# A third kind of first quartic, and one round more between a moved tile's way back and its product

## The chip, the cores and the metric

The kernel runs on one core of one Trainium2 chip. The metric is the device time of one execution in microseconds (us). A core has five engines that each run their own list of instructions in order: the matrix engine (PE; its weight loads are shown apart as PEld), the vector engine (DVE), the scalar engine (ACT), GpSimd (POOL) and SyncE (SP). They wait for each other on semaphores. DMA transfers are issued here from SP and from ACT; the profile shows these issuers as SPq and ACTq.

## The reference, cut to what matters

The input x is 32 images of 32 channels of 128 x 128 numbers in f32. The first layer adds to x the square root, by five Newton steps, of every normalised channel matrix; the second adds a spectral convolution that keeps 32 x 32 modes at two corners.

```python
def _L0_conv_ref(A):
    A2 = A.reshape(b_s * c, n_c, n_c)
    normA = jnp.sqrt(jnp.sum(A2 * A2, axis=(1, 2)))
    Y = A2 / normA[:, None, None]
    Z = jnp.broadcast_to(I, A2.shape)
    for _ in range(5):
        T = 0.5 * (3.0 * I - jnp.matmul(Z, Y))
        Y = jnp.matmul(Y, T)
        Z = jnp.matmul(T, Z)
    return (Y * jnp.sqrt(normA)[:, None, None]).reshape(b_s, c, n_c, n_c)
...
x = x + _L0_conv_ref(_gn(x))
x = x + _L1_conv_ref(_gn(x), L1_conv_weights1, L1_conv_weights2)
```

`_gn` normalises each pair of channels of an image. `_L1_conv_ref` takes the real part of a 2D Fourier transform, mixes 32 input into 32 output channels with a weight for each mode, and transforms back. Most of the matrix work is the first layer: 1024 channel matrices.

## The kernel before, in words

**Sets.** Four channels of an image are a set, so there are 32 x 8 = 256 sets, worked off in order. A set's tile is 128 x 512 (four matrices side by side) and fills one PSUM bank. The kernel holds each matrix and its transpose (`m` and `mb`, loaded as tiles x and b by `fetch`, scaled by `staged`), because PE multiplies the transpose of its first operand.

**Quartics.** Two Newton steps together are a polynomial of degree four, a quartic, in the matrix. `newton` runs, for a set: a first quartic q, y = q times the matrix, the new matrix m = y times q, a second quartic of it, two products with that, a last step t, and a last product that DVE adds to the tile xt. A quartic needs a product, some combination with multiples of the identity, and a second product, whose operands need one more transposition.

There are two ways to get it. `near_quartic` transposes on PE (a matmul with the identity, `transposed`) and uses POOL's sum r = mb + eye; DVE combines PSUM and SBUF into v and w. `far_quartic` has *moved tiles*: DVE transposes 32 x 32 blocks on the way out of PSUM (`turned`, tile turn), and DMAs then put the blocks into their places: `across` with four DMAs of 64 KB inside SBUF, into w; or `away` to DRAM and `back`, one DMA of 256 KB each way. The product reads the result through `by_rows`, in rearranged rows. POOL makes the differences `eye - matrix`. A far set does 10 products of four channels and no PE transposition; a near set does 8 of these, 4 double-width matmuls (`both`) and 3 transpositions of four channels (v twice, m once). Images 1 to 18 are far, image 0 and images 19 (`FIRST`) to 31 are near.

**The order.** The main loop goes in rounds. There are 9 lanes; a lane holds a set's `newton`, a generator, and is advanced by one section, up to its next `yield`, in each round. So a `yield` in a set is one round of the other sets' work between two of its steps. `rest` is two rounds. A new set starts in a free lane when `due` allows, every `FAR` or `NEAR` rounds; near sets also need `room`, under `LESS` = 5 in flight. Once a round the loop also advances the other queues: `preps` (statistics for the normalisation, from xs_in), `posts` (store the finished set to `mid`, the folded sums, the second normalisation), `specs` and `prods` (forward transform and mode products, by groups of 20, 7, 3 and 2 images) and `backs` (the inverse: load `mid` as yt, add, store to out). The order written this way is kept on every engine.

**Buffers.** `rooms` gives for each tag the number of buffers for the whole kernel and of additional ones that exist until `change()`, after `MORE` = 158 sets, gives their memory to the mode products and the inverse. In the late part only the first number is left. When a buffer is used again, its new writer waits for the last reader.

**DMA queues.** `fetch` issues the two loads of a set on SP for far images and on ACT for near ones. Statistics loads are on ACT. Stores to mid and out, loads of yt, spectra and weights, and all moved tiles are on SP. `store` issues out stores whenever it is called and something lies in `stores`, put there by `unfold`, which issues POOL's additions to yt.

All instructions go through one wrapper, so the profile gives line 88 for each: they are told apart by tile names (ps is PSUM).

Of the kernel before, what the change touches and what calls it, by code (L numbers as in the profile page):

```python
# [38 lines left out]
C = 32  # L39
G = 16  # L40
LANES, LESS = 9, 5
FAR, NEAR = 26 / 9, 25 / 5
GROUPS = (20, 7, 3, 2)


# [3 lines left out]
MS = 1 / QR  # L49
# [44 lines left out]
def conv_preact_kernel(  # L94
# [49 lines left out]
        od.append(dram.tile(shape, F32, name=f"od{i}", tag=f"od{i}"))  # L144
    where = [(i, b) for i, n in enumerate(GROUPS) for b in range(n)]

    stp = ctx.enter_context(tc.tile_pool(name="stp", bufs=4))
    up = ctx.enter_context(tc.tile_pool(name="up", bufs=1))
    sp = ctx.enter_context(tc.tile_pool(name="sp", bufs=1))
    small = ctx.enter_context(tc.tile_pool(name="small", bufs=1))  # L150
# [28 lines left out]
    def bank():  # L179
        return ps8.tile([P, 4, P], F32, tag="ps", name="ps")  # L180
# [41 lines left out]
    def prep(bs, made):  # L222
# [5 lines left out]
        tiles = []  # L228
        parts = [(b, i) for b in bs for i in range(C // 4)]

        ahead = 3 if first_b else 8

        def load(k):
            b, i = parts[k]
# [70 lines left out]
        yield  # L305


    rooms = dict(b=(4, 6), xt=(10, 5), x=(3, 2), r=(4, 0), v=(3, 2), w=(3, 2), q=(4, 2))
    rooms.update(my=(4, 3), mb=(2, 4), t=(3, 2), y4=(2, 2), turn=(0, 4))
    turns = dict.fromkeys(rooms, 0)  # L310

    def four(tag, more):
# [44 lines left out]
    def is_far(b):  # L357
        return 0 < b < FIRST
# [16 lines left out]
    def staged(b, g, nm, sc, off, sn):  # L375

        m = four("x", has_more(b, g))
        xt, mb = raw.pop((b, g))

        def on_scalar(t, x, offset, scale, c):  # L380
            c = slice(c, c + 1)
            kept(
                nc.scalar.activation(t, x, AF.Identity, bias=offset[:, c], scale=scale[:, c])
            )

        for j in range(4):
# [20 lines left out]
    def near_quartic(m, mb, more):  # L407


        v = plus(m, -QA * MS, products(mb, m), "v", more)  # L410
        yield
        r = four("r", more)
        nc.gpsimd.tensor_tensor(r, mb, eye, ALU.add)
# [22 lines left out]
        kept(nc.sync.dma_start(out=into, in_=src))  # L436
        return t

    def by_rows(t):
        return blocks(t).rearrange("p a c j -> p c a j")  # L440

    def across(t, more):

        w = four("w", more)
# [7 lines left out]
            )  # L452
        return w

    def far_quartic(m, mb, v, f, later, more):
# [6 lines left out]
        if later:  # L462
# [12 lines left out]
        return q  # L475

    rest = (None, None)

    def newton(g, sn, xt, m, mb, v, far, more):


        qf, et, eye_t = (QS, EYE_Q, eye_q) if far else (QF, EYE, eye)
        if far:
            q = yield from far_quartic(m, mb, v, 1.0, False, more)
        else:
            q = yield from near_quartic(m, mb, more)
        my = four("my", more)
# [23 lines left out]
        else:  # L511
# [2 lines left out]
            mb = taken(transposed(m), "mb", more)  # L514
            yield from rest
            q = yield from near_quartic(m, mb, more)
            both = [bank().rearrange("p (j k) x -> p j k x", k=2) for _ in range(2)]
            for j in range(4):
                nc.tensor.matmul(both[j // 2][:, j % 2], q[:, j], my[:, j], start=True, stop=True)
# [223 lines left out]
    def small_products(i):  # L743
# [121 lines left out]
    def weights():  # L865


        kinds = [("b", 2)] * 3 + [("x", 2), ("b", 4), ("x", 4), ("x", 10)]
        kinds += [("my", 11)] * 2 + [("r", 12)] * 3 + [("mb", 15)] * 2 + [("v", 15)] * 2
        kinds += [("w", 16)] * 2 + [("my", 16), ("r", 17), ("v", 18)] + [("q", 19)] * 3  # L870
# [69 lines left out]
    def unfold():  # L940

        while sums:
            b, o, y, d = sums.pop(0)
            engine = nc.vector if tail and o % 16 else nc.gpsimd
            for half, op in enumerate((ALU.subtract, ALU.add)):
                yh = y[:, :, 64 * half : 64 * half + 64]
                engine.tensor_tensor(yh, yh, d, op)
            stores.append((b, o, y))

    placed = {}  # L950

# [180 lines left out]
    while todo or any(lanes) or posts or specs or prods or backs:  # L1132
# [3 lines left out]
        for i in range(LANES):  # L1136
# [1 line left out]
            step(loads)  # L1138
            far = todo and is_far(todo[0][0])
            under_way = [is_far(lane[0]) for lane in lanes if lane]  # L1140
            room = far or under_way.count(False) + 0.6 * under_way.count(True) < LESS
            if lanes[i] is None and todo and room and rounds >= due:
                due = max(due, rounds - 1) + (FAR if far else NEAR)
                while norms:
                    step(norms)
                b, g = todo.pop(0)
                xt = ready[0][0]
                lanes[i] = (b, g, xt, newton(g, made[b][3], *ready.pop(0), far, has_more(b, g)))
                if stages:
                    stage()  # L1150
                if not todo:
# [89 lines left out]
```

## Time and profile before

| | |
|---|---|
| median of 3 runs | 2969.88 us (2962.28 to 2977.81) |
| the profiled execution, its own time | 2972.83 us |
| its span, first to last instruction | 2971.0 us |
| instructions | 74,313 |
| granted PE clock, mean | 0.987 |
| HBM traffic | 402.42 MB read, 229.11 MB written |
| DMA issues on SP for moved tiles | 288 away, 144 + 144 back, 576 across |

Read along the time axis, the page has four parts. The first 100 us start up with image 0. To about 1500 us the far sets run with almost nothing beside them but statistics and forward transforms. From 1500 us the near sets of images 19 to 31 share the engines with mode products and with the inverse of the first images. After 2850 us the last mode products and inverses run out. Busy shares of each engine by slice stand in the page's second part:

```profile
PE   7999999999999999999999999999999999999995
...
DVE  7779788888788888888886645886787766777565
ACT  3555555555555555555544445555555544655552
POOL 4677777776767777777665534877778764678453
DMA  5687878787787878787843566767767747766577
```

### The profile page before, as it was taken

What the parts mean: (1) busy time and instruction counts of PE and PEld (TensorE: products, weight loads), DVE (VectorE), ACT (ScalarE), POOL (GpSimd) and SP (SyncE); (2) the same over time, 40 slices, a digit from 0 to 9 for tenths busy, and PEclk for the clock granted to TensorE, in tenths of its full rate; (3) what the DMA queues carried; (4) which work ended last, traced back from release to release, by engine and by line L of the source; (5) the groups of instructions that cost most, each with busy time, mean ns of one, the idle gap of its engine ahead of it and who ended that gap; (6) DMA issues with size and microseconds to landing.
All of it is one profiled execution on the core that took longest, in us unless ns stands there. A gap on an engine that the chain in (4) does not pass through costs nothing.

```text
span 2971.0 us, 74313 instructions
## 1 busy us (share of the span) xinstructions
PE 2847.8 (96%) x27688; PEld 2666.9 (90%) x27688; DVE 2270.9 (76%) x4407; ACT 1544.7 (52%) x3899; POOL 1986.9 (67%) x2308
## 2 busy tenths in 40 slices
PE   7999999999999999999999999999999999999995
PEld 7899999998999999999999889888888999888983
DVE  7779788888788888888886645886787766777565
ACT  3555555555555555555544445555555544655552
POOL 4677777776767777777665534877778764678453
PEclk9999999999999999999999999999999999999997
DMA  5687878787787878787843566767767747766577
GB/s 174 185 250 244 242 242 251 240 257 231 233 252 217 275 228 263 236 253 239 270 145 98 164 209 210 269 217 271 269 228 268 273 127 222 218 223 225 180 221 260
DMA packets 553078, 674.22 MB, mean 227 GB/s; under 512 B 99344, under 2 KB 333840, under 8 KB 552720
## 3 DMA queue, kind: packets, MB, share of 16 engines
q1 hardware_dynamic: 480576, 536.53, 56.9%
q10 hardware_dynamic: 72144, 132.94, 14.3%
q8 instruction: 222, 3.64, 0.5%
q14 instruction: 136, 1.11, 0.1%
HBM read 402.42 MB, written 229.11 MB: 213 GB/s over the span
## 4 chain that ended last, share of the span: by engine, by line
PE 66%; POOL 11%; DMA 9%; issue 7%; DVE 5%; ACT 1%; SPq 1%; ACTq 0%; DVEq 0%; POOLq 0%
PE ps L88 66%; POOL yt L88 3%; POOL r L88 3%; POOL x L88 2%; DMA w<-turn 2%; POOL fold L88 2%; DMA yt<-mid 1%; DMA b<-in_x 1%; DMA xt<-in_xt 1%; SPq L88 1%; DVE turn L88 1%; DMA xs<-in_xs 1%; DVE yt L88 1%; DMA mid<-xt 1%; DMA out<-yt 1%
## 5 line engine op out<-in xcount | busy, mean ns | idle before, releaser
L88 ACT ACTIVATE my<-ps 128x512 f32<-128x512 f32 x512 | 305.3, 600 | 563.6 <-PE ps L88 443.7
L88 POOL TENSOR_TENSOR fold<-xt 128x256 f32<-128x256 f32 x512 | 363.5, 732 | 285.9 <-DVE xt L88 257.2
L88 ACT ACTIVATE b<-b,a_off,a_sc 128x128 f32<-128x128 f32 x1024 | 469.8, 493 | 97.1 <-issue 15.9
L88 PE MATMUL ps<-my,q 128*128 128x128 f32 (+1 forms) x2944 | 474.4, 309 | 5.7 <-ACT my L88 3.8
L88 PEld LDWEIGHTS ps<-my,q 128*128 128x128 f32 x2944 | 412.9, 192 | 33.0 <-ACT my L88 4.6
L88 POOL TENSOR_TENSOR v<-eye_v,b 128x512 f32<-128x512 f32 x144 | 183.6, 1275 | 382.9 <-ACT b L88 344.6
L88 POOL TENSOR_TENSOR yt<-yt,d 128x512 f32<-128x512 f32 x244 | 306.8, 1281 | 187.4 <-ACT d L88 155.3
L88 PE MATMUL ps<-w,v 128*128 128x128 f32 x2944 | 399.9, 279 | 13.0 <-DVE w L88 10.6
L88 PEld LDWEIGHTS ps<-w,v 128*128 128x128 f32 x2944 | 363.5, 194 | 22.3 <-issue 7.6
L88 DVE STREAM_TRANSPOSE turn<-ps 128x512 f32<-128x512 f32 x432 | 299.7, 702 | 62.2 <-PE ps L88 57.1
L88 ACT ACTIVATE t<-ps 128x256 f32<-128x256 f32 (+1 forms) x368 | 171.0, 467 | 333.3 <-PE ps L88 316.7
L88 POOL TENSOR_SCALAR x<-xt,a_nm,a_sc 128x128 f32<-128x128 f32 x736 | 321.2, 450 | 15.8 <-DVE a_sc L88 15.5
L88 ACT ACTIVATE y<-ps,a_t_s 128x128 f32<-128x128 f32 x1024 | 291.4, 371 | 45.2 <-PE ps L88 45.1
L88 PE MATMUL ps<-q,t 128*128 128x128 f32 x2048 | 273.8, 277 | 0.8 <-DVE v L88 0.8
L88 DVE SCALAR_TENSOR_TENSOR w<-ps,r 128x512 f32<-128x512 f32 x224 | 153.1, 684 | 139.3 <-POOL r L88 71.2
L88 PEld LDWEIGHTS ps<-q,t 128*128 128x128 f32 x2048 | 249.6, 192 | 3.3 <-issue 1.2
L88 DVE BATCH_NORM_STATS2 a_st<-xs 128x6 f32<-128x256 f32 x504 | 185.9, 410 | 64.9 <-DMA xs<-in_xs 64.6
L88 DVE SCALAR_TENSOR_TENSOR q<-ps,eye 128x512 f32<-128x512 f32 x224 | 153.3, 684 | 97.6 <-PE ps L88 94.8
L88 DVE TENSOR_TENSOR xt<-ps,xt 128x512 f32<-128x512 f32 x256 | 174.7, 683 | 40.7 <-PE ps L88 35.2
L88 POOL TENSOR_TENSOR r<-mb,eye 128x512 f32<-128x512 f32 x112 | 142.9, 1276 | 91.8 <-ACT mb L88 91.8
L88 DVE TENSOR_TENSOR yt<-ps,yt 128x512 f32<-128x512 f32 x256 | 163.3, 681 | 39.9 <-PE ps L88 34.4
L88 POOL TENSOR_TENSOR my<-eye_q,my 128x512 f32<-128x512 f32 x144 | 183.8, 1277 | 7.5 <-PE ps L88 7.5
(147 smaller groups left out, 6284.9 us busy)
## 6 DMA issues: line engine op xcount, KB each, us to landing
turn<-turn SPq DMA_DIRECT2D x288, 256.0 KB
mid<-xt SPq DMA_DIRECT2D x256, 256.0 KB
yt<-mid SPq DMA_DIRECT2D x128, 512.0 KB
xs<-in_xs ACTq DMA_DIRECT2D x252, 256.0 KB
out<-yt SPq DMA_DIRECT2D x115, 512.0 KB
b<-in_x SPq DMA_DIRECT2D x144, 256.0 KB
xt<-in_xt SPq DMA_DIRECT2D x144, 256.0 KB
w<-turn SPq DMA_DIRECT2D x576, 64.0 KB
```

The costliest lines, as they stand in the source:

```text
L88: return self.tc.keep_in_program_order(issue(*args, **kw))
```

## The change

In words: images 19 to 31 get `late_quartic` as their first quartic, with a moved tile instead of the PE transposition (`across`, read five rounds later); their second quartic stays near. The way back in a far set's second quartic is issued four rounds instead of three ahead of its product, and `FAR` goes from 26/9 to 27/9. POOL's sum in `near_quartic` is issued in the section before. Late sets are fetched on SP, half of their m is scaled on ACT instead of POOL, six may be in flight, and out stores are issued two rounds or more after their additions. The buffers are shared out anew; statistics are loaded five tiles ahead instead of three.

```diff
-FAR, NEAR = 26 / 9, 25 / 5
+FAR, NEAR = 27 / 9, 25 / 5
...
-    stp = ctx.enter_context(tc.tile_pool(name="stp", bufs=4))
+    stp = ctx.enter_context(tc.tile_pool(name="stp", bufs=6))
...
-        ahead = 3 if first_b else 8
+        ahead = 5 if first_b else 8
...
-    rooms = dict(b=(4, 6), xt=(10, 5), x=(3, 2), r=(4, 0), v=(3, 2), w=(3, 2), q=(4, 2))
-    rooms.update(my=(4, 3), mb=(2, 4), t=(3, 2), y4=(2, 2), turn=(0, 4))
+    rooms = dict(b=(5, 5), xt=(10, 4), x=(3, 2), r=(3, 0), v=(3, 2), w=(3, 2), q=(3, 3))
+    rooms.update(my=(3, 4), mb=(2, 4), t=(2, 3), y4=(2, 2), turn=(2, 2))
...
     def fetch(b, g):
-        queue = nc.sync if is_far(b) else nc.scalar
+        queue = nc.sync if b else nc.scalar
...
-            if j < 2 or not is_far(b):
+            if j < 2 or not b:
...
     def near_quartic(m, mb, more):
-        v = plus(m, -QA * MS, products(mb, m), "v", more)
-        yield
         r = four("r", more)
         nc.gpsimd.tensor_tensor(r, mb, eye, ALU.add)
+        v = plus(m, -QA * MS, products(mb, m), "v", more)
+        yield
         yield
         w = plus(transposed(v), 1.0, r, "w", more)
...
+    def late_quartic(m, mb, more):
+        v = minus(eye_v, m, four("v", more))
+        ps = products(mb, m)
+        t = turned(ps, more)
+        yield
+        nc.vector.scalar_tensor_tensor(v, ps, 1 / (9 * MS), v, ALU.mult, ALU.add)
+        w = across(t, more)
+        yield
+        minus(eye_q, mb, mb)
+        yield from rest
+        yield from rest
+        q = plus(products(v, by_rows(w)), 9 / (39 * MS**2), mb, "q", more)
+        yield from rest
+        return q
...
     def far_quartic(m, mb, v, f, later, more):
...
         if later:
             w = back(held, "w", more)
-            yield
+            yield from rest
         yield from rest
...
         if far:
             q = yield from far_quartic(m, mb, v, 1.0, False, more)
+        elif late:
+            q = yield from late_quartic(m, mb, more)
         else:
             q = yield from near_quartic(m, mb, more)
...
         for k2 in range(len(xks)):
             load_spectra(k2)
+        yield from rest
...
     def store():
-        while stores:
-            b, o, y = stores.pop(0)
+        while stores and (tail or rounds - stores[0][3] >= 2):
+            b, o, y, _ = stores.pop(0)
...
-            room = far or under_way.count(False) + 0.6 * under_way.count(True) < LESS
+            less = LESS if any(under_way) else LESS + 1
+            room = far or under_way.count(False) + 0.6 * under_way.count(True) < less
...
             if i == 3 or tail:
                 step(posts)
+            if i == 0:
+                store()
```

Left out are the passing on of `late`, the constants that go with it (QS and EYE_Q for the first half of a late set, QF and EYE after), and a new list of slots into which `weights` loads the last weights as buffers come free.

More of the change, by code (lines that the diff above doesn't have):

```diff
@@ L407, in near_quartic @@
     def near_quartic(m, mb, more):
+        r = four("r", more)
+        nc.gpsimd.tensor_tensor(r, mb, eye, ALU.add)
         v = plus(m, -QA * MS, products(mb, m), "v", more)
         yield
-        r = four("r", more)
-        nc.gpsimd.tensor_tensor(r, mb, eye, ALU.add)
         yield
@@ L437, in back @@
         return t
-    def by_rows(t):
-        return blocks(t).rearrange("p a c j -> p c a j")
     def across(t, more):
@@ L453, in across, with by_rows @@
         return w
+    def by_rows(t):
+        return blocks(t).rearrange("p a c j -> p c a j")
+    def late_quartic(m, mb, more):
[12 more added lines that the diff above has]
+        return q
     def far_quartic(m, mb, v, f, later, more):
@@ L459, in far_quartic @@
             held = away(turned(ps, more))
+            yield
         else:
             w = across(turned(ps, more), more)
-        if later:
-            yield
         nc.vector.scalar_tensor_tensor(v, ps, 1 / (9 * MS), v, ALU.mult, ALU.add)
@@ L477, in conv_preact_kernel, with newton @@
     rest = (None, None)
-    def newton(g, sn, xt, m, mb, v, far, more):
-        qf, et, eye_t = (QS, EYE_Q, eye_q) if far else (QF, EYE, eye)
+    def newton(g, sn, xt, m, mb, v, far, late, more):
+        qf, et, eye_t = (QS, EYE_Q, eye_q) if far or late else (QF, EYE, eye)
         if far:
             q = yield from far_quartic(m, mb, v, 1.0, False, more)
+        elif late:
+            q = yield from late_quartic(m, mb, more)
         else:
@@ L516, in newton @@
             q = yield from near_quartic(m, mb, more)
+            qf, et, eye_t = QF, EYE, eye
             both = [bank().rearrange("p (j k) x -> p j k x", k=2) for _ in range(2)]
@@ L865, in weights @@
     def weights():
-        kinds = [("b", 2)] * 3 + [("x", 2), ("b", 4), ("x", 4), ("x", 10)]
-        kinds += [("my", 11)] * 2 + [("r", 12)] * 3 + [("mb", 15)] * 2 + [("v", 15)] * 2
-        kinds += [("w", 16)] * 2 + [("my", 16), ("r", 17), ("v", 18)] + [("q", 19)] * 3
+        kinds = [("b", 3)] * 3 + [("x", 3), ("b", 6), ("x", 6), ("b", 10), ("x", 12)]
+        kinds += [("my", 13)] + [("r", 14)] * 2 + [("mb", 17)] * 2 + [("v", 17)] * 2
+        kinds += [("w", 18)] * 2 + [("my", 18), ("r", 19), ("v", 20), ("y4", 21)] + [("q", 21)] * 2 + [("q", 23)]
         first = B * C // 4 - 10
@@ L947, in unfold @@
                 engine.tensor_tensor(yh, yh, d, op)
-            stores.append((b, o, y))
+            stores.append((b, o, y, rounds))
     placed = {}
@@ L1147, in conv_preact_kernel @@
                 xt = ready[0][0]
-                lanes[i] = (b, g, xt, newton(g, made[b][3], *ready.pop(0), far, has_more(b, g)))
+                lanes[i] = (b, g, xt, newton(g, made[b][3], *ready.pop(0), far, b >= FIRST, has_more(b, g)))
                 if stages:
```

## The prediction

> **What bounds the kernel now.** I read the page's busy times first, then stages of the span, then the timeline of the matrix engine alone, then the waits.
>
> ```profile
> PE 2847.8 (96%) x27688; PEld 2666.9 (90%) x27688; DVE 2270.9 (76%) x4407; ACT 1544.7 (52%) x3899; POOL 1986.9 (67%) x2308
> ...
> PE 66%; POOL 11%; DMA 9%; issue 7%; DVE 5%; ACT 1%; SPq 1%; ACTq 0%; DVEq 0%; POOLq 0%
> ```
>
> PE is busy nearly all the time, and the chain of waits that ended last lies on it for two thirds. Matmuls overlap, though, so 96% may hide slack. The stages (length; then busy PE, PEld, DVE, ACT, POOL; granted clock, DMA share, GB/s) and a stretch of PE alone:
>
> ```profile
> 100.00:1500.00 1400.00, 1362.79 (x12287) 1318.56 (x12286) 1173.71 (x2303) 756.90 (x1929) 1023.89 (x1138) 0.99 0.80 244
> 1500.00:1900.00 400.00, 391.66 (x4071) 361.66 (x4071) 257.87 (x511) 191.59 (x476) 204.97 (x274) 1.00 0.55 175
> 1900.00:2850.00 950.00, 924.53 (x9851) 842.89 (x9850) 695.51 (x1294) 505.36 (x1278) 663.24 (x784) 0.99 0.68 225
> ```
>
> ```profile
> 2254.83 1.16 PE L88 MATMUL ps<-y,t 128*128 128x128 f32 x8
> 2255.82 1.06 PE L88 MATMUL ps<-my,mb 128*128 128x128 f32 x8
> 2256.71 0.60 PE L88 MATMUL ps<-ident,v 128*128 128x128 f32 x4
> 2257.15 2.78 PE L88 MATMUL ps<-my,q 128*128 128x256 f32 x16
> ```
>
> Read the starts, not the lengths. A four-channel product is 8 records (two for each f32 matmul) and the next group starts 0.89 us later, 0.112 a record. A transposition of four channels is 4 records and takes 0.44 us. If each record is charged its usual start-to-start step, of the 2971 us some 166 are left that are not matrix work: 63 in 100 to 1500 us (images 1 to 18), 18 in 1500 to 1900, 47 in 1900 to 2850, the rest at start and end. PE works through its list with 4 to 5% of gaps in either main stage, so work taken from it should come off the end time.
>
> What the gaps are:
>
> ```profile
> DVE w L88 <- POOL r L88: 71.2, 35, 5.6
> ...
> PE ps L88 <- DMA w<-turn: 17.2, 11, 5.2
> ```
>
> (us in total, times, longest.) The first is DVE waiting for POOL's sum in the near quartics; the late products of w and v lose 13.1 us against their usual step. The second is PE itself, waiting for a moved tile. It falls on products that read w and r, the second quartic of the far sets; with the shorter gaps that go by other names, those products lose 26.5 us between 100 and 1500 us.
>
> **The change, part by part.**
>
> *First quartic of images 19 to 31.* It drops one transposition: 13 images x 8 sets x 4 = 416 transposing matmuls.
>
> ```profile
> L88 PE MATMUL ps<-ident,v 128*128 128x128 f32 x896 | 137.9, 277 | 4.5 <-DVE xt L88 2.3 <-DVE v L88 2.2
> L88 POOL TENSOR_SCALAR x<-xt,a_nm,a_sc 128x128 f32<-128x128 f32 x736 | 321.2, 450 | 15.8 <-DVE a_sc L88 15.5 <-DMA xt<-in_xt 0.3
> L88 ACT ACTIVATE x<-xt,a_off,a_sc 128x128 f32<-128x128 f32 x288 | 143.6, 499 | 9.5 <-DVE xt L88 2.5 <-DMA mb<-turn 2.4 <-DVE v L88 2.3
> L88 POOL TENSOR_TENSOR v<-eye_v,b 128x512 f32<-128x512 f32 x144 | 183.6, 1275 | 382.9 <-ACT b L88 344.6 <-PE ps L88 35.8 <-ACT b_r L88 2.5
> L88 DVE STREAM_TRANSPOSE turn<-ps 128x512 f32<-128x512 f32 x432 | 299.7, 702 | 62.2 <-PE ps L88 57.1 <-DMA w<-turn 1.1 <-DMA mb<-turn 0.2
> L88 DVE SCALAR_TENSOR_TENSOR w<-ps,r 128x512 f32<-128x512 f32 x224 | 153.1, 684 | 139.3 <-POOL r L88 71.2 <-PE ps L88 57.8 <-POOL x L88 8.5
> ```
>
> The 277 ns are the length of one, overlapping its neighbours; the starts give 0.109, so 416 x 0.109 = 45 us off PE. Bounds: 50 (the mean step with waits is 0.119), and 0 if PE were not the bound. I take -45. The product that stays reads its moving operand in rearranged rows; the far sets' products do so already at the same 0.112, so nothing is added.
>
> The Trainium skill (TensorE: Matmul & The Clock Gate, Part 4: PE-mode transpose) gives about 275 ns for a 128x128 transposition inside a kernel, the length that this row shows too. By it the part would bring 416 x 0.275 = 114 us; the starts, which decide, bring 45.
>
> Per late set the other engines get: POOL two differences of 1.275 for one sum of 1.276 and two scalings of 0.450 fewer, +0.375 us, 39 us over 104 sets; ACT two scalings, +1.0 us; DVE a transposition (0.702) and a combination (0.65) for two combinations (0.682 and 0.684), nothing. In 1900 to 2850 us POOL is busy for 0.70, ACT 0.53, DVE 0.73; idle time covers all three. If it did not, the POOL part would cost up to 39 us.
>
> SP gets four issues of 64 KB per late set (their issue lasts 0.594 us at the median in the far stage, 2.4 us a set of 13) and the two loads of a set that ACT's queue had (statistics loads stay on ACT's). What is queued behind on SP is the store of the finished set, the y loads and stores of the inverse, and late weights. The DMA engines get 512 pieces of 512 bytes. In the far stage such a piece takes 29 ns, so 512 x 29 / 16 = 0.93 us a set, 0.07 on a share of 0.68: 0.75, still under the 0.80 of the far stage.
>
> The Trainium skill (DMA: Bandwidth & Descriptors, Rules for kernel authors) speaks against this: many small transfers should be coalesced, and its bandwidth table (Measured) has 0.95 us for 64 KB. By that, four would fill the DMA engines for 3.8 us of a set's 13 and bring the share to 0.97, where every late load waits; the pieces in the trace are four times cheaper, and the page's own next section limits the penalty of small pieces to HBM.
>
> *Is the moved tile there in time?* The product stands five rounds behind its issue. Adding PE's records (at the steps above) in the built order between issue and product gives 8.9 us at least and 11.0 at the median. In the far stage of the trace before, pieces of w landed, counted from their place in the order, after 6.6 us (half), 9.9 (90%), 11.5 (98%), 13.5 (last); issue lag on SP is in it. A few late sets wait some 2 us: +4, from 0 to 45.
>
> *Way back of the far sets, 27 rounds.* The product goes from three rounds behind the issue to four. The same count: median from 9.8 to 11.6 us, the shortest 2% from 6.5 to 9.8. Against the landings above, the 10% that came too late become about 2%. Of 26.5 us I take 15 back; bounds 0 (the wait reappears elsewhere) and 26.5. A lane is held one round longer, 28 for 27, so nine lanes start a set every 3.1 rounds instead of 3.0; a round has no work of its own, so PE's list is as long as before. DVE-fed products come slightly closer (median of the nearest 4.9 for y and q in both).
>
> *Second quartic's sum on POOL one section earlier; shorter late rounds.* The sum is now two rounds ahead of its reader: up to 13 us back. But a late round holds less PE work: late products with a DVE or ACT producer 1.5 to 3 us ahead rise from 73 to 266. In the trace before, products at 2 to 3 us lost 0.02 us each, those at 3 to 4 us 0.08: 193 x 0.08 = 15 us at most. In the first quartic DVE's combination now waits for POOL's difference, one round behind it, as it waited for the sum; queued behind it on DVE are the other sets' q, w and t, and PE for those: the same kind of wait as the 35 above, no more of them. Together +2, from -13 to +15.
>
> *The rest:* stores two rounds later on SP (SP waited 195.0 us for POOL's y between 1900 and 2850; nothing PE needs soon was behind it), deeper statistics loads (DVE waited 64.6 us for xs, off PE's path), regrouped buffers (the closest reuse, POOL's v, comes 2.9 us of PE work after its last reader), a sixth late set in flight, two idle rounds before small products, other weight slots: 0, covered by gaps on SP, ACT and DVE. Were that cover gone, DVE's 64.6 us is the largest of these. The last set passes two more rounds; five other sets cover most of them: +1, at most 5.
>
> **Sum.** 2971.0 - 45 - 15 + 4 + 2 + 1 = 2918. The profiled run took 2972.8, 1.8 around its span, and the median of the runs is 2.9 under it: 2917.
>
> **Rivals.**
> *Slower: SP's late queue.* The four moves stand behind y loads of 512 KB. In the trace those landed 8.6 us (half) and 12.5 (90%) after their place. If the moves land like them, a quarter of 104 sets is some 3 us late, +78 us: 2971 - 45 - 15 + 78 + 1 - 1 = 2989. It decides from 0.6 us of lateness per late set on average. For it: loads moved to the same queue. Against: DMA share below the far stage's, delayed stores that stop blocking SP.
> *Nothing from PE:* the late rounds are paced by DVE and POOL, and the removed transpositions become gaps. Only the far part stays: 2971 - 15 + 1 - 1 = 2956. For it: PEld idle for 0.11 late, and nearer producers. Against: 5 us of gaps per 100.
> *More:* the far and late waits go whole: 2971 - 50 - 26 - 13 - 1 = 2881; half of that surplus, 2899, is likelier.
>
> **How the numbers follow.** Forecast 0.64, more 0.12, nothing from PE 0.14, slower 0.10. The predicted time is 2917. The range 2895 to 2953 leaves out most of the slower rival, the edge of "nothing from PE" and the far end of "more". About 0.5%, or 15 us, is what a measurement tells from no change. Faster (under 2955): 0.64 + 0.12 + 0.05 of the third = 0.81; same 0.09 of it + 0.02 = 0.11; slower 0.08.
>
> **What would show it.** Right: products from ident and v fall from 896 to 480 records with unchanged step; PE's wait for w<-turn falls below 5 us in the far stage though more w pieces are moved; 1500 to the end is 40 us shorter. Wrong: PE waits for w<-turn after 1500 us (first rival); PE's gaps per 100 us grow from 5 to 8 there under DVE's names (second); or the far stage is no shorter.

## The result, and the profile after

| | before | after |
|---|---|---|
| median of 20 runs each | 2967.89 us (2959.00 to 2977.81) | 2974.85 us (2961.55 to 2992.61) |
| ratio after/before | | 1.0031, 95% interval 1.0018 to 1.0043 |
| span of the profiled run | 2971.0 us | 2982.5 us |
| sets 9 to 152 (far) | 1429.5 us | 1447.6 us |
| sets 153 to 256 (late) | 1342.9 us | 1332.3 us |
| after the last set | 65.5 us | 70.1 us |

The change costs about 9 us: slower by 0.3%, within what the prediction counted as no change. The forecast of 2917 us and its whole range were on the other side. (A stage ends here where DVE adds the last product of its last set to xt. One profile is one execution; runs of one kernel spread over some 20 us, and e14 and e12 below, with the same far part, differ by 17 us in its length; so a stage length says little below that. Ratios decide.)

The page's busy times and its chain that ended last, after:

```profile
PE 2823.2 (95%) x27272; PEld 2632.7 (88%) x27272; DVE 2289.9 (77%) x4409; ACT 1612.1 (54%) x4107; POOL 2024.9 (68%) x2202
...
PE 61%; DMA 13%; DVE 9%; POOL 7%; issue 5%; ACT 2%; SPq 2%; ACTq 0%; DVEq 0%; POOLq 0%
```

PE has 416 records fewer and is busy 24.6 us less, yet the span is 11.5 us longer: the work went, and waits came. In the chain PE's share fell from 66% to 61%. The stages after (columns as in the prediction):

```profile
100.00:1500.00 1400.00, 1349.24 (x12112) 1302.09 (x12111) 1169.65 (x2273) 745.82 (x1906) 1005.47 (x1117) 0.99 0.78 240
1500.00:1900.00 400.00, 379.16 (x3882) 350.14 (x3881) 245.16 (x490) 206.77 (x522) 211.38 (x239) 0.98 0.62 189
1900.00:2850.00 950.00, 910.10 (x9623) 825.05 (x9618) 718.74 (x1323) 558.49 (x1438) 704.16 (x726) 0.99 0.79 250
```

In all three PE is busy for less of the same time, by 14, 12.5 and 14 us. In the first, where no PE work was taken out, that is loss alone: 12,112 records got through where there had been 12,287. DMA's share from 1900 to 2850 us went from 0.68 to 0.79, more than the 0.75 expected. Charging every record its usual step, as the prediction did, gives these gaps (an estimate): 78.7 us in the far stage (before 57.9), 104.5 in the late one (75.7) and 23.9 after it (19.3). What PE waited for from 100 to 1500 us (us in total, times, longest), three lines of before and then those of after, and below them one line of after from 1900 to 2850 us:

```profile
PE ps L88 <- ACT z L88: 4.5, 3, 2.1
...
PE ps L88 <- ACT my L88: 0.4, 1, 0.4
PE ps L88 <- POOL fold L88: 0.3, 1, 0.3
```

```profile
PE ps L88 <- ACT z L88: 13.0, 5, 7.5
PE ps L88 <- DMA w<-turn: 7.1, 8, 1.7
PE ps L88 <- DVE q L88: 6.0, 7, 2.6
PE ps L88 <- ACT my L88: 5.0, 2, 3.4
PE ps L88 <- POOL fold L88: 4.8, 4, 2.5
```

```profile
PE ps L88 <- DMA w<-turn: 1.3, 3, 0.7
```

The moved tiles do nearly what was forecast: the far sets' wait for w fell from 17.2 to 7.1 us (the sign was "below 5"), and the late ones come in time. In their place stand waits for ACT, DVE and POOL, engines that are 54, 77 and 68% busy. The groups that the first part was costed by, with the sum r of before on top:

```profile
L88 POOL TENSOR_TENSOR r<-mb,eye 128x512 f32<-128x512 f32 x112 | 142.9, 1276 | 91.8 <-ACT mb L88 91.8
```

```profile
L88 PE MATMUL ps<-ident,v 128*128 128x128 f32 x480 | 74.0, 277 | 4.6 <-DVE v L88 4.6
...
L88 DVE STREAM_TRANSPOSE turn<-ps 128x512 f32<-128x512 f32 x536 | 375.5, 705 | 153.9 <-PE ps L88 143.7
...
L88 POOL TENSOR_TENSOR r<-mb,eye 128x512 f32<-128x512 f32 x112 | 142.9, 1276 | 224.9 <-ACT mb L88 213.9
```

The transpositions left at an unchanged length. POOL's sum r, issued one section earlier, now stands at the head of POOL's queue until ACT has copied mb: 91.8 us of waiting before, 213.9 after.

### The profile page after: what moved, and what is told of

Same layout as the page of the kernel before. It is cut to its first block, busy times and chain, and to the rows that moved or that the text cites. A ratio compares the mean times of both kernels' runs of the same rounds, so it can differ in the third digit from the quotient of the medians.

```text
span 2982.5 us, 74465 instructions
## 1 busy us (share of the span) xinstructions
PE 2823.2 (95%) x27272; PEld 2632.7 (88%) x27272; DVE 2289.9 (77%) x4409; ACT 1612.1 (54%) x4107; POOL 2024.9 (68%) x2202
## 4 chain that ended last, share of the span: by engine, by line
PE 61%; DMA 13%; DVE 9%; POOL 7%; issue 5%; ACT 2%; SPq 2%; ACTq 0%; DVEq 0%; POOLq 0%
PE ps L88 61%; DMA w<-turn 3%; SPq L88 2%; POOL yt L88 2%; DMA yt<-mid 1%; POOL fold L88 1%; DVE turn L88 1%; POOL x L88 1%; DMA mid<-xt 1%; DVE yt L88 1%; DMA xt<-in_xt 1%; DVE root L88 1%; DMA out<-yt 1%; DMA mb<-turn 1%; DVE q L88 1%
## 5 line engine op out<-in xcount | busy, mean ns | idle before, releaser
L88 ACT ACTIVATE b<-b,a_off,a_sc 128x128 f32<-128x128 f32 x1024 | 486.8, 497 | 54.6 <-DMA xs<-in_xs 23.6
L88 DVE STREAM_TRANSPOSE turn<-ps 128x512 f32<-128x512 f32 x536 | 375.5, 705 | 153.9 <-PE ps L88 143.7
L88 POOL TENSOR_TENSOR r<-mb,eye 128x512 f32<-128x512 f32 x112 | 142.9, 1276 | 224.9 <-ACT mb L88 213.9
L88 ACT ACTIVATE x<-xt,a_off,a_sc 128x128 f32<-128x128 f32 x496 | 248.9, 502 | 20.4 <-DMA xs<-in_xs 8.6
L88 POOL TENSOR_SCALAR x<-xt,a_nm,a_sc 128x128 f32<-128x128 f32 x528 | 232.7, 451 | 14.7 <-DVE a_sc L88 14.7
L88 DVE BATCH_NORM_STATS2 a_st<-xs 128x6 f32<-128x256 f32 x504 | 184.3, 408 | 15.4 <-DMA xs<-in_xs 15.4
L88 DVE BATCH_NORM_STATS2 b_st<-xt 128x6 f32<-128x256 f32 x512 | 186.6, 404 | 0.1
```

The source lines that it names most:

```text
L88: return self.tc.keep_in_program_order(issue(*args, **kw))
```

## The experiments

All ratios are to the kernel before, measured on the same chip as each. A difference of two of them is uncertain by some 7 us, by their intervals. Stages (far, late, tail) are from the one profile of each.

| kernel | ratio, 95% interval | far | late | tail |
|---|---|---|---|---|
| changed kernel | 1.0031 (1.0018 to 1.0043) | 1447.6 | 1332.3 | 70.1 |
| e1_far26 | 1.0063 (1.0041 to 1.0085) | 1422.5 | 1358.7 | 68.2 |
| e2_nolate | 1.0064 (1.0042 to 1.0086) | 1445.5 | 1329.8 | 75.4 |
| e3_before27 | 1.0098 (1.0072 to 1.0123) | 1457.4 | 1343.5 | 67.3 |
| e4_fetchact | 1.0084 (1.0060 to 1.0108) | 1442.0 | 1345.5 | 69.9 |
| e5_regular | 1.0035 (1.0021 to 1.0048) | 1418.8 | 1355.8 | 75.3 |
| e6_dummy | 1.0398 (1.0375 to 1.0421) | 1441.4 | 1434.2 | 69.6 |
| e7_shift | 1.0075 (1.0056 to 1.0094) | 1425.9 | 1347.0 | 74.6 |
| e8_before_reg | 0.9923 (0.9902 to 0.9944) | 1401.5 | 1340.6 | 63.9 |
| e9_lane27 | 1.0024 (1.0008 to 1.0040) | 1411.7 | 1357.3 | 67.9 |
| e10_r_back | 1.0047 (1.0032 to 1.0062) | 1413.6 | 1358.4 | 69.7 |
| e11_buffers | 0.9951 (0.9933 to 0.9969) | 1417.0 | 1336.0 | 65.6 |
| e12_lean | 0.9973 (0.9954 to 0.9992) | 1391.5 | 1356.4 | 66.5 |
| e13_stats | 0.9948 (0.9931 to 0.9965) | 1401.0 | 1353.5 | 68.6 |
| e14_pe_lean | 1.0034 (1.0019 to 1.0049) | 1408.4 | 1374.7 | 67.6 |
| e15_pe_e8 | 0.9979 (0.9966 to 0.9991) | 1404.4 | 1364.6 | 64.0 |
| e16_near45 | 0.9928 (0.9910 to 0.9947) | 1395.7 | 1332.4 | 89.9 |
| e17_near475 | 0.9947 (0.9926 to 0.9968) | 1395.2 | 1336.9 | 79.4 |
| e18_e8_475 | 0.9918 (0.9898 to 0.9938) | 1399.8 | 1320.1 | 83.9 |

### The far part undone, and the far part alone

e1 is the changed kernel with the far sets' old distance and spacing; e3 is the kernel before with the new ones.

```diff
 # e1, against the changed kernel; e3 is the reverse, against the kernel before
-FAR, NEAR = 27 / 9, 25 / 5
+FAR, NEAR = 26 / 9, 25 / 5
...
             w = back(held, "w", more)
-            yield from rest
+            yield
```

> The changed kernel with the far part alone undone: FAR back to 26/9 and the second quartic's product three rounds behind the way back. In the changed kernel's trace the first image and the far sets ended at 1580.0 us instead of 1562.6, 17 later, with as much matrix work. Theory A (the extra round costs more than the wait it hides): that stage is short again, 2975 - 17 = 2958 us, ratio 0.997. Theory B (the forecast: the extra round hides waits for moved tiles, and the 17 us come from the buffers, the deeper statistics loads or one odd execution): 2975 + 10 to 15 = 2985 to 2990 us, ratio 1.006 or more, and PE's waits for w<-turn in the far stage rise from 7 to about 17 us.

> The kernel before with the far part alone: FAR 27/9 and the second quartic's product four rounds behind the way back. Theory A: 2968 + 17 = 2985 us, ratio 1.006. Theory B (forecast): 2968 - 15 = 2953, ratio 0.995, and PE's waits for w<-turn fall from 17 to under 7 us.

Alone (e3) the far part costs 1.0%, some 29 us, nearly all of it in the far stage. Undone in the changed kernel (e1) it gives the far stage 25 us back, as theory A had it, but the late stage takes 26 more and the time is worse: that it lands on theory B's 1.006 is chance. So the far part as written slows its own stage, though its aim is met: in e3 the products of w and r lose 7.5 us instead of 26.5. What else changed there is when sets start. Before, one started every 3 rounds exactly; with a lane held for 28 rounds, nine lanes give 3, 3, ... and then 4.

### The same distance with regular starts

e8 is e3 with the lane given back in the round of the set's last product, so that it is held 27 rounds.

```diff
         nc.vector.tensor_tensor(xt, ps, xt, ALU.add)
...
-        yield
+        if not far:
+            yield
```

> The kernel before with the far part alone and the lane given back in the round of the last product, so that sets start every 3 rounds exactly. Theory A1 (irregular starts cost it): the far stage falls from the 1457 us of e3_before27 to 1430 - 15 = 1415 us, the whole to 2968 - 15 = 2953, ratio 0.995. Theory A2: the far stage stays near 1450, ratio 1.007 or more.

e8 is 0.8% faster than the kernel before, and 1.7%, some 52 us, faster than e3, from which this line alone separates it. The stage line from 100 to 1500 us, of e3 and then of e8, and what PE waited for there in e3:

```profile
100.00:1500.00 1400.00, 1349.72 (x12091) 1301.71 (x12090) 1173.47 (x2270) 743.70 (x1896) 1002.06 (x1112) 0.99 0.78 239
```

```profile
100.00:1500.00 1400.00, 1382.45 (x12547) 1339.32 (x12547) 1192.53 (x2362) 759.39 (x1961) 1044.15 (x1158) 1.00 0.80 247
```

```profile
PE ps L88 <- DVE q L88: 10.0, 9, 3.4
PE ps L88 <- ACT z L88: 8.9, 3, 5.4
PE ps L88 <- DMA w<-turn: 5.5, 5, 2.1
PE ps L88 <- POOL fold L88: 5.0, 5, 3.2
PE ps L88 <- DVE w L88: 3.5, 1, 3.5
```

With even starts PE is busy for 33 us more of the same 1400. Its gaps in the far stage are 84.7 us in e3 and 31.3 in e8; before the change they were 57.9. No single wait explains e3: products of b and q lose 15.4 us against 5.7, those of z 10.6 against 1.2, of t and y 8.1 against 0.6. That giving the lane back a round earlier is worth this much is shown. But it does three things at once: starts become even, they come every 3.0 rounds instead of 3.1, and the finished set's store and sums follow a round sooner. Which of them pays was not separated; that rounds with one set fewer hold less PE work between a producer and its reader is argued only. Below, e17 and e18 start late sets every 4.75 rounds, so after 5, 5, 5 and 4 in turn, and are no slower than with an even 5.

### In the changed kernel: regular starts, and the side work moved by a round

e5 is the changed kernel with e8's line, and the side work (statistics, products, inverse), which is dealt out by the number of the round, shifted by one. e9 has e8's line alone; e7 is e1 with the shift alone.

```diff
 # e5 and e7
-            if i == 1 and (early or rounds % 2):
+            if i == 1 and (early or (rounds + 1) % 2):
...
-            turn = rounds % 10 in (0, 3, 7)
+            turn = (rounds + 1) % 10 in (0, 3, 7)
```

> The changed kernel, but a far set gives its lane back in the round of its last product (its last yield dropped), so that nine lanes hold it 27 rounds and a set starts every 3 rounds exactly, as before, while the product stays four rounds behind the way back. Late sets then start one round earlier against the ten-round rhythm of mode products and inverse; that rhythm is moved by one round too, so that they stand to it as in the changed kernel. Theory A1 (the far stage lost its 18 us because 28 rounds on nine lanes make the starts irregular, 3 3 3 4): the far stage takes 1422 us or less instead of 1448 and the whole 2975 - 25 = 2950 us, ratio 0.995. Theory A2 (the longer stay itself, or any product four rounds behind, costs it): 2975 as it is, ratio 1.003, far stage over 1440.

> The kernel with the far part undone (e1_far26), and the ten-round rhythm of mode products, inverse and statistics moved by one round, so that late sets stand to it as in the changed kernel. Theory of alignment (e1_far26 lost 26 us after 1580 us only because its late sets start one round earlier against that rhythm): the stage from the 152nd set on shrinks from 1427 to about 1400 us and the whole to 2984 - 26 = 2958, ratio 0.998. If alignment is nothing: 2984, ratio 1.006.

> The changed kernel with one edit only: a far lane is free in the round of its last product, so far sets start every 3 rounds exactly (e5 had besides this the side work moved by one round). Theory 'regular starts': the far stage is about 1419 us as in e5 (changed kernel 1448), the time is 2978 or less. Rival 'the moved side work was what spoilt e5': 2955 to 2967, late sets plus tail at least 12 us shorter than e5's 1431. If the lane were only worth something beside the shift, it would stay at 2975 with a far stage of 1448.

The far stage is 29 us (e5) and 36 us (e9) shorter, as with e8, but the time hardly follows: 1.0035 and 1.0024 against 1.0031. The late stage gives most of it back, with the shift or without. e7's time is no better than e1's. So a shift of the side work by one round is not the reason. Part of what is longer can be named. PE's wait for POOL's fold from 1600 to 2900 us, in the changed kernel, e5 and e9:

```profile
PE ps L88 <- POOL fold L88: 3.8, 5, 1.8
```

```profile
PE ps L88 <- POOL fold L88: 24.0, 12, 2.7
```

```profile
PE ps L88 <- POOL fold L88: 17.4, 10, 2.7
```

It is 17.6 us in e1 and 22.4 in e7, whose late stages are longer too, and under 2 before the change and with the old quartic (e2, e3 and e8). So it comes where the whole late part meets regular far sets; without the parts around the quartic (e12, below) it is 2.3. Why it comes there stays open.

### Which of the other parts costs

e10 is e9 with POOL's sum back in its old place. e11 is e8 with the changed kernel's buffers and statistics loads. e12 is e10 without the parts around the late quartic. e13 is e9 with the old statistics loads alone.

```diff
 # e13, against e9
-    stp = ctx.enter_context(tc.tile_pool(name="stp", bufs=6))
+    stp = ctx.enter_context(tc.tile_pool(name="stp", bufs=4))
...
-        ahead = 5 if first_b else 8
+        ahead = 3 if first_b else 8
```

```diff
 # e10, against e9 (near_quartic)
-        r = four("r", more)
-        nc.gpsimd.tensor_tensor(r, mb, eye, ALU.add)
         v = plus(m, -QA * MS, products(mb, m), "v", more)
         yield
+        r = four("r", more)
+        nc.gpsimd.tensor_tensor(r, mb, eye, ALU.add)
         yield
```

```diff
 # e12, against e10; besides these, e13's two lines and no store() at i == 0
-        while stores and (tail or rounds - stores[0][3] >= 2):
+        while stores:
...
-            less = LESS if any(under_way) else LESS + 1
+            less = LESS
...
             load_spectra(k2)
-        yield from rest
```

```diff
 # e11, against e8: the changed kernel's rooms, weights() list, and
-    stp = ctx.enter_context(tc.tile_pool(name="stp", bufs=4))
+    stp = ctx.enter_context(tc.tile_pool(name="stp", bufs=6))
...
-        ahead = 3 if first_b else 8
+        ahead = 5 if first_b else 8
```

> e9 with POOL's sum r of the second quartic back in its old place, one section later. Theory 'POOL in order': put early, r waits at the head of POOL for ACT's copy mb (91.8 us of such waits before, 213.9 changed) and delays fold and yt behind it, for which PE waits; put back, the waits return to about 90 us and the time falls by 8 to 20 us against e9. Rival 'r is not on the path': within 4 us of e9. Third: r then comes too late for w, DVE waits for it again (71.2 us before), 5 to 10 us slower than e9.

> e8 (the kernel before with the far part and regular starts) with the changed kernel's buffers alone: its counts of each tile, six statistics buffers with five loads ahead, and its list of tiles for the late weights; the late sets keep their old quartic. Theory 'other buffers': they explain the far stage's 1401.5 us in e8 against 1418.8 in e5, so 2955 to 2962 here with a far stage of 1415 or more. Rival 'buffers cost nothing': within 4 us of e8's 2942.

> e10 without the parts around the late quartic: output stores issued at once again, no sixth late set, no extra section ahead of the spectrum products, four statistics buffers with three loads ahead. What is left is the far part, regular starts, the late quartic, its buffers and SP as the late sets' queue. Theory 'the parts around it cost': 2930 to 2950, at or below e8. Rival 'the late quartic gives back what it saves in PE work': within 6 us of e10, with PE gaps after 1500 us still 25 us or more above e8's.

> e9 (changed kernel, lane free in the round of its last product) with four statistics buffers and three loads ahead, as before the change. Theory 'statistics loads five ahead slow the far stage': the far stage falls from e9's 1412 us to 1392 to 1400 and the time from 2972 to about 2957. Rival 'it was the stores, the sixth set or the extra section': within 5 us of e9, far stage 1405 or more.

The statistics loads are the find: two numbers bring e9 from 1.0024 to 0.9948, some 22 us, with intervals far apart. e12's gain over e10 is no larger, and it has them too; without a sixth set its late sets start unevenly, nearly all after 4 to 6 rounds, so it says little on the rest, and neither of its expectations came. e11 points the same way, 8 us and 15 us of far stage, but its interval overlaps e8's. POOL's sum is better early: e10 is slower than e9, so the third theory held there: DVE waits for r again, 44.8 us in all. POOL's wait for ACT's mb fell from 191.2 to 82.7 us as the first one said, but that did not decide the time.

Five loads ahead do what they are for. DVE's wait for xs from 200 to 1500 us, in e9 and in e13:

```profile
DVE a_st L88 <- DMA xs<-in_xs: 3.0, 4, 1.4
```

```profile
DVE a_st L88 <- DMA xs<-in_xs: 27.1, 27, 1.8
```

The kernel that waits nine times longer is the faster one: DVE had the time. Part of what they cost shows on ACT, which issues them. e11's timeline of ACT and its issuing queue, and of PE (start, length, in brackets the idle time before and what ended it), then the windows around it (PE's clock is the third number from the end):

```profile
647.25 0.60 ACT L88 ACTIVATE my<-ps 128x512 f32<-128x512 f32 x1 [3.23 <-PE ps L88]
647.27 5.44 ACTq L88 DMA_DIRECT2D xs<-in_xs  x5
652.76 0.88 ACT L88 ACTIVATE b<-b,a_off,a_sc 128x128 f32<-128x128 f32 x2 [4.92 <-DMA xs<-in_xs]
...
657.03 0.65 ACT L88 COPY z<-ps 128x256 f32<-128x256 f32 x2
```

```profile
657.74 1.11 PE L88 MATMUL ps<-ident,z 128*128 128x128 f32 x4 [4.01 <-ACT z L88]
```

```profile
653.70:657.70 4.00, 0.03 (x1) 0.00 (x0) 1.35 (x3) 3.98 (x12) 1.97 (x2) 0.78 0.99 311
657.10:660.50 3.40, 2.76 (x13) 2.77 (x14) 0.00 (x0) 2.20 (x5) 2.34 (x2) 0.50 0.84 256
```

Issues of the next images' loads stand in a burst. Four went out by 649.5 us, a fifth at 652.4, and until then ACT did nothing: it takes its queue in order. The trace shows what held the fifth. It waits on a semaphore that it shares with a moved tile that SP had issued at 647.39 us; the tile's last piece landed at 652.36, and the load went out at 652.38. The sixth went out at 655.98, with another move on its semaphore landed at 655.96. ACT's scalings and its copy z came late, PE stood for 4.0 us before the transposition of z, and then ran at half clock until 662.8 us: its products, else 0.89 us apart, started 1.70 us apart. e11 has three such gaps before z above 1 us (1.5, 2.5 and 4.0 us), e9 two (2.2 and 4.0), e8 and e13 none. That is one mechanism, seen; it accounts for a part of the 22 us, not for all: PE's waits for z from 200 to 1500 us are 6.7 us in e9 and 1.6 in e13. And ACT's stops before statistics loads in the far stage, nearly all of which end with a landing on the load's semaphore, come to 42.4 us in e9 and 38.9 in e13, so depth adds little to their sum. Where the rest of the 22 us arises is not shown.

### Is it PE's list that sets the late stage?

e6 added a discarded transposition of v to the late quartic of the changed kernel. It cost 4%, but not as PE work: v is read there a round after DVE's combination, so PE waited 80.2 us for DVE's v.

```diff
 # e6, against the changed kernel (late_quartic)
         yield
+        transposed(v)
         minus(eye_q, mb, mb)
```

> The changed kernel with four transposing matmuls put back into each late first quartic, whose result nobody reads (the output is unchanged): PE has the 45 us of work again, and nothing else is as before. If PE's list sets the late time: 2975 + 45 = 3020 us, ratio 1.018. If the late stage is paced by the time between a product and the DVE or ACT result that the next one needs (second rival): PE's gaps give way to the dummies, 2975 + 0 to 10, ratio 1.003 to 1.007, and the gaps after 1580 us fall from about 109 to about 70 us. In between, 2995, if half of it is covered.

e14 and e15 add the same number of transpositions, 416, of a constant, at the start of each late set; nothing reads them. e14 does so to e12, which has the late quartic, e15 to e8, which does not.

```diff
 # e14 against e12, e15 against e8
+    def idle():
+        ps = bank()
+        for j in range(4):
+            nc.tensor.transpose(ps[:, j, :], ident, ident)
...
                 lanes[i] = (b, g, xt, newton(...))
+                if b >= FIRST:
+                    idle()
```

> e12 plus four transpositions of a constant tile at the start of each late set, which nobody waits for and nobody reads: 416 x 0.109 us = 45 us of PE work put back. Theory 'late sets are paced by waits between engines, PE's saved work became gaps': at most 15 us slower than e12's 2957, PE gaps after 1500 us 30 us smaller. Rival 'PE's list still sets the end': 40 to 50 us slower.

> The same 416 idle transpositions added to e8, whose late sets are those before the change. Theory 'PE's list set the late stage before the change, and no longer after it': 35 to 45 us slower than e8's 2942. If the late sets were paced by waits before the change already, under 20 us slower.

45 us of PE work cost 18 us with the new quartic (0.9973 to 1.0034) and 17 with the old (0.9923 to 0.9979), each give or take 7. e15 was expected to be the contrast, and is not: with the old quartic too PE's list sets the late pace only in part. After set 152 to the end, where 43 of the 45 us are added, e15 takes 24 us more than e8, and e14 19 more than e12: the rest, 19 and 24 us, went into gaps that were there. So what is added to a PE that is 97% busy partly fills its gaps. That what is taken from it opens gaps in the same measure, so that the 45 us were worth some 17 from the start, is inferred; the kernel before itself was not tried. The page's line of e8, and then of e15:

```profile
PE 2839.0 (97%) x27688; PEld 2659.3 (90%) x27688; DVE 2264.2 (77%) x4407; ACT 1535.4 (52%) x3899; POOL 1992.3 (68%) x2308
```

```profile
PE 2874.3 (97%) x28104; PEld 2696.4 (91%) x28104; DVE 2263.5 (76%) x4407; ACT 1535.1 (52%) x3899; POOL 1991.1 (67%) x2308
```

### What the late quartic is worth

e2 is the changed kernel with the old quartic for the late sets. e4 gives their loads back to ACT's queue.

```diff
 # e2
-... newton(g, made[b][3], *ready.pop(0), far, b >= FIRST, has_more(b, g)))
+... newton(g, made[b][3], *ready.pop(0), far, False, has_more(b, g)))
 # e4
-        queue = nc.sync if b else nc.scalar
+        queue = nc.sync if is_far(b) else nc.scalar
```

> The changed kernel with images 19 to 31 on the near quartic for both halves; everything else as changed. PE gets its 416 transpositions back (45 us of work). If PE's list sets the late part's time: 2975 + 45 = 3020 us. If what the trace shows is right (the late part got 11 to 16 us shorter, the rest of the 45 went into new gaps of PE): 2975 + 11 to 16 = 2986 to 2991. If late rounds are paced by other engines (second rival): 2975, and PE's gaps after 1580 us fall by about 45 us.

> The changed kernel with the late images' two loads a set back on ACT's queue. If SP's queue is what holds up the late part (mode products waited 15.2 us for plain<-xs instead of 4.9, and SP's issues lag by 1 to 3 us more than before): 2975 - 15 = 2960 us, ratio 0.998. If it isn't: 2975 within 5, ratio 1.001 to 1.005.

In the changed kernel the quartic brings 10 us (1.0064 to 1.0031), give or take 7, a quarter of its PE work. SP is the better queue for the loads by 16 us (e4), so the first rival, SP's late queue, falls as it was put: behind those loads the moved tiles were in time. But PE's wait for plain<-xs, spectra that SP loads for the mode products, is 15.2 us from 1600 to 2900 in the changed kernel, 4.9 before, 15.9 in e4 and 0.9 in e2: it comes with the new quartic and not with the loads of the sets. Whether SP's moves cause it is not shown.

With regular starts the quartic and the parts around it, together, bring nothing; the quartic alone was not tried there. e13 has all of the change but the lane and the statistics loads, e8 the far part alone: 0.9948 against 0.9923, and PE's gaps after set 152 grow from 104.5 to 167.4 us, more than the 45 us of work that left. PE's waits from 1500 to 2900 us, in e8 and then in e13:

```profile
PE ps L88 <- POOL fold L88: 1.9, 3, 0.8
PE ps L88 <- DMA plain<-xs: 1.8, 2, 1.0
```

```profile
PE ps L88 <- POOL fold L88: 20.4, 12, 2.7
PE ps L88 <- DMA plain<-xs: 14.3, 7, 3.9
```

and what POOL itself stood for there, in e8 and in e13:

```profile
POOL fold L88 <- DVE xt L88: 236.2, 62, 13.5
...
POOL r L88 <- ACT mb L88: 73.5, 27, 10.0
```

```profile
POOL r L88 <- ACT mb L88: 184.5, 47, 9.0
...
POOL fold L88 <- DVE xt L88: 72.2, 38, 5.4
POOL b L88 <- PE ps L88: 24.8, 18, 6.4
```

In e8 POOL came to a fold before its data and waited; in e13 the data wait for POOL, and PE waits for the fold. That POOL is late because it stands at r, or at the new difference in b, is argued: e10 showed that r alone is not the cure, and the changed kernel, whose POOL stands longer at r, has 3.8 us of PE's waits for folds. Fold and plain<-xs together are 31 of the 63 us by which the gaps grew.

e16 to e18 put more late sets in flight: a start every 4.5 or 4.75 rounds, six sets allowed. e16 is e12 with 4.5, e17 is e13 with 4.75, e18 is e8 with 4.75.

```diff
-LANES, LESS = 9, 5
-FAR, NEAR = 27 / 9, 25 / 5
+LANES, LESS = 9, 6
+FAR, NEAR = 27 / 9, 19 / 4
```

> e12 with late sets started every 4.5 rounds instead of 5 and six allowed at once. Theory 'too little PE work between a producer and its reader': more sets in flight lengthen the distance, the gaps after 1500 us shrink by 15 us or more and the time falls to 2925 to 2945. Rival 'the late sets wait for their own engines or for buffers however many fly': within 6 us of e12, or slower because the products and inverses, which are served by the round, get 52 rounds fewer and fall into the tail (tail above 80 us).

> e13 (all of the change, lane free in the round of its last product, statistics loads as before the change) with late sets started every 4.75 rounds and six allowed at once. Theory 'late sets need more in flight to use the smaller PE list': 2930 to 2945, 10 us or more below e13's 2956 and at or below e8's 2942. Rival 'e16's gain over e12 came from fewer rounds whatever the quartic': then e18 gains as much over e8 and stays ahead of this kernel by 10 us or more.

> e8 (kernel before, far part, regular starts, old late quartic) with the same closer late starts, every 4.75 rounds. Theory 'with the old quartic PE had work enough between producer and reader': within 5 us of e8's 2942. Rival 'closer starts help any late quartic': 2925 to 2935.

e16 gains 13 us over e12, but e12's irregular starts go at the same time (e16's are 5 and 4 rounds in turn). e17 gains nothing over e13, e18 nothing over e8: what the late stage wins the tail loses (e18: 20.5 us against 20). e18 keeps 0.9918 without the late quartic, e17 0.9947 with it. These intervals overlap, as do those of e8 and e13; both pairs point to the old quartic, and neither shows any gain from the new one. e16, with it, lies between (0.9928). The best kernels here, e8 and e18 (2941.59 and 2938.23 us), are 0.8% faster than the kernel before and carry none of the late part.

## Why the prediction was wrong, step by step

The forecast was 53 us below the median shown; the runs are 9 above theirs. By ratios, building up from the kernel before:

| step | forecast | measured |
|---|---|---|
| far distance, with regular starts (e8) | -15 | -23 |
| late quartic and what goes with it (e8 to e13) | -45 + 4 + 2 = -39 | +7 |
| statistics loads five ahead (e13 to e9) | 0 | +22 |
| lane held 28 rounds (e9 to the changed kernel) | 0 | +2; +52 without the late part (e8 to e3) |

Only -23, +22 and +52 are clear of the noise; +7 and +2 are not. The forecast's tail (+1) is not measured by itself; the measured column adds up to +8. The steps are not independent, as the last row shows, so another order of building would divide them otherwise.

- *"A round has no work of its own, so PE's list is as long as before."* True, and it decided nothing: with as much matrix work, a lane held for 28 rounds instead of 27 costs 52 us in the kernel before (e8 to e3), through uneven or through thinner rounds. The term of -15 priced that at nothing. The distance itself was right in mechanism: the products' loss fell from 26.5 to 10.6 us, and with regular starts to 0.7; its size was too small.
- *"So work taken from it should come off the end time."* This step carried 45 of the 53 us. It was read from a PE with 4 to 5% of gaps. Taken out, the work brought 10 us in the changed kernel (e2), and nothing with what goes with it after regular starts (e13); put back, as much work costs 17 or 18. The rival "nothing from PE", at 0.14, came closest: most of the transpositions became gaps. Its sign, PE gaps growing from 5 to 8 per 100 us, came: after set 152 from 6.7 (95.0 of 1408) to 9.2 (128.4 of 1402). The names were not DVE's alone, but DMA's plain<-xs (4.9 to 15.2 us from 1600 to 2900), POOL's and ACT's too.
- *"POOL +0.375 us a set ... idle time of all three covers it."* By busy shares it does, and in the changed kernel PE's waits for folds rose only from 1.8 to 3.8 us. With regular starts they are 17 to 24 us; that POOL, which takes its queue in order, then stands at r, b or v while folds are ready is argued.
- *"Deeper statistics loads ...: 0, covered by gaps."* They cost 22 us. The cover was counted for DVE, which waits for the loads, and not for ACT, which issues them; ACT's stops are seen to cost a part, the rest stays open.
- *Is the moved tile there in time: +4.* Right: 1.3 us of waits after 1900 us, and the SP rival as it was put fell with it.
- *Usual step 0.109 of a transposition:* right. The Trainium skill's 275 ns (TensorE: Matmul & The Clock Gate, Part 4) agree with the length of one (277 ns here); taken as its price they would have put the forecast further off.
- *More issues on SP, their cost:* none for the moved tiles themselves, but PE's wait for plain<-xs, which SP loads too, grew by 10 us and is gone without the new quartic (e2).

## What to carry to other kernels

A busy share near 100% on the bounding engine does not say that its work sets the time: before pricing a saving, add the same amount of idle work to the kernel there is, and expect no more than that slope (here 17 of 45 us, and the removal itself brought 10 or nothing). In a software pipeline, check that lanes times spacing equals the rounds that a lane is held: one round too many cost 52 us. An operation or a load that is put earlier on an in-order queue is priced by what then stands behind it, not by the idle share of the engine.

## What the runs showed of the hardware

An engine that issues transfers can be stopped by another engine's transfers for far longer than an issue lasts: four issues of 256 KB on ACT's queue took 0.37 to 0.79 us each, the fifth came 2.9 us after the fourth had ended, 0.02 us after a move of SP's on the same semaphore had landed, and ACT's own work stood for 4.9 us.

A PE gap can be paid twice. Around the 4.0 us gap above the trace's clock record has half rate from 655.9 to 662.8 us, 5.0 us of it after PE had resumed. Over the whole span such pieces took 40.0 us of PE's clock before the change (half of their length), 52.9 after, 31.8 in e8; 16 to 22 us of each lie after 2880 us. The Trainium skill (TensorE: Matmul & The Clock Gate, Part 1) says that half rate comes after an idle window of about 3.4 us and lasts until a busy one. The end agrees. The start does not: half rate came 2.2 us after PE's last matmul, with PE busy for 1.2 us of the 3.4 before it, so here a shorter gap was enough.
